# Layer 0's routing logits as eight extra columns of the value and output projections, without the transposes of the second norm

## The chip, the core and the metric

The kernel runs on one core of a Trainium2 chip. The metric is the device time of one execution in microseconds, the median over runs. TensorE is called PE here (its weight loads, which run beside matmuls, PEld), VectorE DVE, ScalarE ACT, GpSimd POOL and SyncE SP; SP issues the DMAs of this kernel. Everything is float32 unless noted. An fp32 matmul leaves two matmul records in the trace, a transpose one.

## What is computed

The reference is a network of two layers on x of shape (2, 256, 56, 56). Only layer 0 matters here:

```python
x = x + attention(_ln_c(x), wq, bq, wk, bk, wv, bv, wo, bo)   # 7x7 windows, 8 heads of 32, _ln_c: over channels, eps 1e-6
t = _to_tokens(x)                                             # 6272 tokens of 256
u = _ln_t(t)                                                  # over channels, eps 1e-5
logits = u @ router_w.T                                       # 8 experts
...
rw, re = jax.lax.top_k(softmax(logits), 2)                    # renormalised
t = t + u + sum_e combine[:, e] * (gelu(u @ w1[e] + b1[e]) @ w2[e] + b2[e])
```

Layer 1, two 3x3 convolutions with ternary weights and a second mixture of experts, has its own code after it.

## The kernel before

`metaformer` is the path that runs; `general` stands behind a flag for inputs that it doesn't cover. The picture is cut into 14 strips (`STRIPS`, 2 images of 7) of 8 rows, a strip has 448 tokens (`NT`), that is 4 tiles (`NTT`) of 112 tokens (`TT`, 8 rows by 14 columns). The 256 channels `C` are two halves (`KC`) of 128 partitions, `E` is 8.

**The attention stage** loops over strips g, over 4 column tiles and 2 channel halves. Each of the 8 steps of a strip does `scores` (`sc`, a matmul per head, L1435, and a mask, L1444; ACT turns them into `ex`, L1454), then `attend` for the step before (`av`, L1464; DVE adds it to `acc`, L1474). Beside them generators advance by one `yield` a step:

- `project(g + 2)`: `token_stats` (DVE L700 to L705, POOL L713 to L715 gives `rstd` and `nmr`), `scaled` on ACT (`xn`, L721), eight transposes `px` (L1375) copied by ACT to `xc`, then the keys and queries `pj` (L1387; ACT writes `keys`, DVE `q_im`, L1399), one yield each, and the values `pv` (L1409) in two steps of two token tiles: two outputs of 112x256 in one PSUM tile, two DVE adds into `vals` (L1417).
- `leave(g - 1)`: `again` loads the strip a second time as `xr` and adds the output bias on POOL (L1320); the softmax's sums go out and come back by DMA (`sums`, `den`, `shares`, `rec`); DVE builds `oc` (L1520); then the last projection `pw` (L1533), two token tiles to a PSUM tile, and DVE adds it to `xr` (L1541). Then `norm0`, the second normalisation: `token_stats` of `xr`, ACT makes `u` (L721), eight transposes `pu` (L763) are copied by ACT to `ut` (L768), POOL adds u to xr (L770) and SP stores it as `x_mid`, eight matmuls `pl` of N = 8 (L777, 16 records) give the logits, and DVE copies them to `lgs` (L788).
- `settle0`, once both strips of a pair are normalised: DVE picks the best two experts (`first_max`: `most`, `hot`, `at`, L804 to L808), PE ranks tokens (`rk`, L836), DVE places them (`place`, `pos`, L858), and POOL scatters the rows to the experts' lists (`xs`, L860, 16 indirect DMAs a pair).

PSUM: `px`, `pj`, `pv`, `pw`, `pu`, `pl`, `rk` share one tag, `aux`, of pool `att_ps` with two buffers of one bank; `sc` and `av` have six banks of their own. A tile is handed out again when its last reader is done.

The order of instructions on each engine in the attention stage comes from the framework's scheduler. The expert stages are in an order written out by hand for SP, DVE, PE and ACT (`experts_in_order`). Strips 12 and 13 are "late": the rest of their `leave` runs between the tiles of layer 0's experts (`beside(j)` moves each generator by a step for each expert tile, and `routed_all` plans the remaining tiles after the last), and they use DVE where the other strips use POOL.

Of the kernel before, what the change touches and what calls it, by code (L numbers as in the profile page):

```python
# [20 lines left out]
P = 128  # L21
# [55 lines left out]
def bcast(ap, axis, shape):  # L77
    return ap.unsqueeze(axis).to_broadcast(shape)
# [551 lines left out]
def metaformer(ctx: ExitStack, tc: tile.TileContext, a: dict, out: bass.AP, flag):  # L630
# [88 lines left out]
    def scaled(dest, src, rstd, nmr):  # L719
        for t in range(NTT):  # L720
            nc.scalar.activation(  # L721
                dest[:, t, :],
                src[:, t, :],
                AF.Identity,
                bias=nmr[:, t : t + 1],
                scale=rstd[:, t : t + 1],
            )

    def routing(layer, wp, tp, ps):

        pre = f"L{layer}_ffn_"
        gate = wp.tile([P, KC, E], F32, tag="gate", name="gate")
        nc.sync.dma_start(gate, a[pre + "gate"].rearrange("(k p) e -> p k e", p=P))
        if layer == 1:
            gate_b = wp.tile([TT, E], F32, tag="gate_b", name="gate_b")
            nc.sync.dma_start(gate_b, a[pre + "gate_b"].partition_broadcast(TT))
# [11 lines left out]
        def norm(i, src, late=False):  # L748


            eng = nc.vector if late else small_eng
# [5 lines left out]
            scaled(u, src, rstd, nmr)  # L757
            yield
# [10 lines left out]
            if layer == 0:  # L769
                eng.tensor_tensor(src, src, u, ALU.add)  # L770
                nc.sync.dma_start(x_mid[i], src)
                yield
            lg = lgs[:, i * NTT : (i + 1) * NTT, :]
            pl = ps.tile([TT, NTT, E], F32, tag="pl" if layer else "aux", name="pl")
# [9 lines left out]
            if layer == 1:  # L784
                yield
                nc.vector.tensor_tensor(lg, pl, bcast(gate_b, 1, [TT, NTT, E]), ALU.add)
            else:
                nc.vector.tensor_copy(lg, pl)  # L788
# [209 lines left out]
        return norm, settle, tiles, gates, wgt, counted, sent  # L998
# [294 lines left out]
    with ExitStack() as st:  # L1293
# [22 lines left out]
        def again(g, eng):  # L1316

            xr[g] = tp.tile([TT, NTT, C], F32, tag="xr", name="xr")
            nc.sync.dma_start(xr[g], a["x_tok"][g])
            eng.tensor_tensor(xr[g], xr[g], bcast(bias["o"], 1, [TT, NTT, C]), ALU.add)  # L1320

# [3 lines left out]
        for n in "kqvo":  # L1325
            wt[n] = (aw if n == "o" else sw).tile([P, KC, C], F32, tag=f"w{n}", name=f"w{n}")
            nc.sync.dma_start(wt[n], a[f"L0_conv_w{n}"].rearrange("(k p) o -> p k o", p=P))
# [15 lines left out]
        nc.vector.tensor_copy(far_w.rearrange("p h w -> p (h w)"), far_f)  # L1343
        fits = aw.tile([TT, DEN], F32, tag="fits", name="fits")
# [5 lines left out]
        def fresh(s):  # L1350


            rows = slice(s * SR, (s + 1) * SR)
            nc.sync.dma_start(acc[:, :, rows, :], bcast(a["fresh"][:, rows, :], 1, [P, PAIRS, SR, W]))
# [8 lines left out]
        norm0, settle0, tiles0, gates0, wgt0, counted0, _ = routing(0, aw, tp, ps)  # L1363

        def project(g):
# [39 lines left out]
            for t in range(0, NTT, 2):  # L1405
                pj = ps.tile([TT, 2, C], F32, tag="aux", name="pv")
                for i in range(2):
                    for k in range(KC):
                        nc.tensor.matmul(  # L1409
                            pj[:, i, :],  # L1410
                            xc[:, k, (t + i) * TT : (t + i + 1) * TT],
                            wt["v"][:, k, :],
                            start=k == 0,
                            stop=k == KC - 1,
                        )
                for i in range(2):
                    nc.vector.tensor_tensor(  # L1417
                        vals[g % 3][:, t + i, :, 0::3, :],
                        pj[:, i, :].rearrange("p (j i d) -> p j i d", i=2, d=HD),
                        bias["v"].rearrange("p (j i d) -> p j i d", i=2, d=HD),  # L1420
                        ALU.add,
                    )
                yield
# [54 lines left out]
        def leave(g):  # L1478
# [50 lines left out]
            for t in range(0, NTT, 2):  # L1529
                pw = ps.tile([TT, 2, C], F32, tag="aux", name="pw")  # L1530
                for i in range(2):
                    for k in range(KC):
                        nc.tensor.matmul(  # L1533
                            pw[:, i, :],
                            oc[:, k, (t + i) * TT : (t + i + 1) * TT],
                            wt["o"][:, k, :],
                            start=k == 0,
                            stop=k == KC - 1,
                        )
                x = xr[g][:, t : t + 2, :]  # L1540
                nc.vector.tensor_tensor(x, pw, x, ALU.add)  # L1541
# [28 lines left out]

        fresh(0)
# [3 lines left out]
        finish(project(1))  # L1575
        before = None
# [105 lines left out]
    with mid:  # L1682
# [133 lines left out]
        with ExitStack() as both:  # L1816
# [45 lines left out]
            norm, settle, tiles, gates, wgt1, _, sent = routing(1, wp, tp, ps)  # L1862
# [115 lines left out]
def _laid_out(inputs):  # L1978
# [16 lines left out]
    for n in "qkvo":  # L1995
        a[f"L0_conv_w{n}"] = i[f"L0_conv_w{n}"].T
        a[f"L0_conv_b{n}"] = per_channel(i[f"L0_conv_b{n}"])
    a["L0_ffn_gate"] = i["L0_ffn_router_w"].T
# [61 lines left out]
```

## Time and profile before

| | us |
|---|---|
| median of 3 runs | 1784.78 |
| all runs | 1784.78, 1773.98, 1792.38 |
| profiled execution | 1925.16 (span 1923.3, granted clock 0.866) |
| busy over the span | PE 1564.4, PEld 1224.5, DVE 927.7, ACT 711.4, POOL 668.5 |
| scatters `xs` on POOL, both layers | 224 of 0.954 mean, 213.7 in all |

The profiled execution took 140.38 us more than the median of the runs. The profile of the whole span in 40 slices of 48 us:

```profile
PE   6999787797868875995789899966447999999964
...
PEclk9999798897968987997899999955557999999975
DMA  7032233212136676786653000033363787878758
```

Each digit is the busy share of a slice in tenths; PEclk is the clock that PE was granted. The attention stage covers the first 11 or 12 slices, layer 0's experts follow to about slice 19, then come the convolutions and layer 1's experts. The rows of the page that belong to the work around the change are groups of instructions: line, engine, operation, output and inputs, shapes, count; then busy time and mean ns of one; then the idle time just before them and what ended it.

```profile
L1409 PE MATMUL pv<-wv,xc 128*112 128x256 f32 x224 | 54.7, 388 | 0.0
L763 PE MATMUL pu<-ident,u 112*128 112x112 f32 x112 | 14.4, 270 | 0.0
L1541 DVE TENSOR_TENSOR xr<-pw,xr 112x512 f32<-112x512 f32 x28 | 19.3, 688 | 20.7 <-PE pw L1533 20.6
L1417 DVE TENSOR_TENSOR vals<-pv,bv 112x256 f32<-112x256 f32 x56 | 21.1, 417 | 27.2 <-PE pv L1409 27.2
```

Matmuls are pipelined, so the mean of one in such a row overstates what it holds PE for; the busy sum is the one to use.

### The profile page before, as it was taken

How to read it: one execution, taken by the hardware profiler on the slowest of the kernel's cores; microseconds unless marked ns; L12 is line 12 of the kernel's file. 1: busy time of each engine (PE TensorE's matmuls, PEld its weight loads, DVE VectorE, ACT ScalarE, POOL GpSimd, SP SyncE). 2: the span in 40 equal slices, each digit the busy share in tenths (PEclk: the TensorE clock that was granted, in tenths of full speed). 3: DMA queues.
4: the chain of work that ended last, by engine and by line, in shares of the span. 5: the costliest groups of instructions: out<-in, count | busy, mean ns of one | idle time of the engine just before them, and what ended most of it. 6: DMA issues, size and time to landing. Idle time of an engine off the chain costs nothing.

```text
span 1923.3 us, 26006 instructions
## 1 busy us (share of the span) xinstructions
PE 1564.4 (81%) x8709; PEld 1224.5 (64%) x8709; DVE 927.7 (48%) x2621; ACT 711.4 (37%) x1388; POOL 668.5 (35%) x676
## 2 busy tenths in 40 slices
PE   6999787797868875995789899966447999999964
PEld 3555454454537764784678788855335888888852
DVE  4467355354644425884787555575533111111136
ACT  3454332342323423542655352244223333333312
POOL 3013433414133564443355234235554222222210
PEclk9999798897968987997899999955557999999975
DMA  7032233212136676786653000033363787878758
GB/s 235 21 90 77 89 101 96 73 44 69 31 109 217 214 245 231 262 291 196 170 153 101 0 1 1 1 103 105 92 200 111 250 278 264 270 271 275 273 170 289
DMA packets 91887, 291.79 MB, mean 152 GB/s; under 512 B 20487, under 2 KB 35803, under 8 KB 80416
## 3 DMA queue, kind: packets, MB, share of 16 engines
q1 hardware_dynamic: 66736, 231.79, 38.3%
q0 software_dynamic: 21200, 51.82, 7.7%
q10 hardware_dynamic: 3808, 6.42, 1.0%
q8 instruction: 71, 1.16, 0.2%
q14 instruction: 72, 0.59, 0.1%
HBM read 218.51 MB, written 74.20 MB: 152 GB/s over the span
## 4 chain that ended last, share of the span: by engine, by line
PE 60%; DVE 14%; DMA 8%; issue 7%; another core or an unknown queue 6%; ACT 3%; POOL 2%; SPq 1%; DVEq 0%; POOLq 0%; ACTq 0%
PE ph L1091 13%; PE py L1108 12%; PE pc L1753 10%; PE av L1464 5%; PE pj L1387 4%; PE sc L1435 3%; DMA got<-ys 3%; PE pw L1533 3%; PE pv L1409 2%; PE pt L1059 2%; PE pl L777 2%; DVE t_stats L700 1%; DMA x_on<-x_mid 1%; PE pu L763 1%
## 5 line engine op out<-in xcount | busy, mean ns | idle before, releaser
L1091 PE MATMUL ph<-ut,w 128*128 128x256 f32 (+1 forms) x1472 | 317.6, 367 | 12.5 <-issue 6.5
L1108 PE MATMUL py<-w,h 128*128 128x256 f32 x1288 | 299.9, 381 | 2.4 <-issue 2.4
L1116 DVE TENSOR_TENSOR y<-py,w 128x512 f32<-128x512 f32 (+1 forms) x120 | 76.8, 640 | 441.7 <-PE py L1108 388.2
L1091 PEld LDWEIGHTS ph<-ut,w 128*128 128x128 f32 x1472 | 255.7, 198 | 43.9 <-issue 8.7
L860 POOL DMA_INDIRECT xs<-u,pos x224 | 213.7, 954 | 162.6 <-issue 97.7
L1753 PE MATMUL pc<-hi,wq 128*128 128x448 f32 x672 | 255.4, 381 | 16.6 <-ACT hi L1724 16.6
L1108 PEld LDWEIGHTS py<-w,h 128*128 128x128 f32 x1288 | 245.3, 192 | 36.0 <-issue 2.8
L1753 PE MATMUL pc<-lo,wq 128*128 128x448 f32 x672 | 254.1, 379 | 0.0
L1118 POOL DMA_INDIRECT ys<-y,dest x136 | 136.2, 1002 | 272.1 <-DVE dest L1066 186.4
L1098 ACT ACTIVATE h<-ph,w 128x256 f32<-128x256 f32 (+1 forms) x368 | 162.2, 448 | 129.0 <-PE ph L1091 74.1
L1454 ACT ACTIVATE ex<-sc 112x476 f32<-112x476 f32 (+3 forms) x224 | 116.7, 570 | 245.7 <-PE sc L1444 166.2
L1063 ACT COPY ut<-pt 128x512 f32<-128x512 f32 (+1 forms) x120 | 65.2, 543 | 308.3 <-PE pt L1059 246.0
L1474 DVE TENSOR_TENSOR acc<-av,acc 128x238 f32<-128x238 f32 (+3 forms) x224 | 87.6, 407 | 154.1 <-PE av L1464 72.4
L1464 PE MATMUL av<-ex,vals 112*64 112x238 f32 (+3 forms) x896 | 130.7, 413 | 28.6 <-DVE acc L1474 21.8
L1723 POOL TENSOR_TENSOR v<-pad 128x928 f32<-128x928 f32 (+1 forms) x56 | 98.3, 1761 | 159.4 <-DVE lo L1725 146.7
L1753 PEld LDWEIGHTS pc<-hi,wq 128*128 128x128 f32 x672 | 128.5, 192 | 31.8 <-ACT hi L1724 17.9
L1753 PEld LDWEIGHTS pc<-lo,wq 128*128 128x128 f32 x672 | 128.7, 192 | 15.4 <-DVE lo L1725 1.0
L1118 POOL DMA_INDIRECT ys<-y,to x81 | 84.4, 1042 | 127.3 <-DVE dest L1066 65.8
L1435 PE MATMUL sc<-q_im,keys 32*112 32x238 f32 (+3 forms) x896 | 99.3, 439 | 32.5 <-ACT ex L1454 21.2
L1464 PEld LDWEIGHTS av<-ex,vals 112*64 112x64 f32 x896 | 57.4, 146 | 83.5 <-issue 37.9
L713 POOL TENSOR_TENSOR t_rstd<-t_mv,eps 112x4 f32<-112x4 f32 x26 | 5.3, 203 | 280.9 <-DVE t_mv L702 280.9
L1724 ACT CAST hi<-v 128x928 fp32r<-128x928 f32 x56 | 54.1, 966 | 109.7 <-PE pc L1753 103.9
(237 smaller groups left out, 2286.1 us busy)
## 6 DMA issues: line engine op xcount, KB each, us to landing
w<-in_L_experts SPq DMA_DIRECT2D x64, 1154.0 KB
w<-in_L_experts SPq DMA_DIRECT2D x56, 641.0 KB
xg<-xs SPq DMA_DIRECT2D x97, 260.0 KB
got<-ys SPq DMA_DIRECT2D x28, 896.0 KB
acc<-in_fresh SPq DMA_DIRECT2D x14, 896.0 KB
xt<-in_x_tok SPq DMA_DIRECT2D x14, 448.0 KB
xr<-in_x_tok SPq DMA_DIRECT2D x14, 448.0 KB
rec<-shares SPq DMA_DIRECT2D x28, 224.0 KB
```

The source lines that it names most:

```text
L860: w = nc.gpsimd.indirect_dma_start(xs[:, :], bass.IndirectOffsetOnAxis(ap=pos[:, j, t0 + t : t0 + t + 1], axis=0), us[t // NTT][:, t % NTT ...
L1091: nc.tensor.matmul(ph[:, :g], w1[:, k, f * P : (f + 1) * P], d["ut"][:, k, :g], start=k == 0, stop=k == KC - 1,)
L1098: nc.scalar.activation(d["h"][:, f, :g], ph[:, :g], AF.Gelu, bias=b1[:, f : f + 1])
L1108: nc.tensor.matmul(py[:, i, :], d["h"][:, f, i * P : (i + 1) * P], w2[:, f, :], start=f == 0, stop=f == NF - 1,)
L1118: o = nc.gpsimd.indirect_dma_start(ys[:, :], bass.IndirectOffsetOnAxis(ap=d["to"][:, i : i + 1], axis=0), y[:, i, :], None, bounds_check=T ...
L1387: nc.tensor.matmul(pj[:, :NT], wt[n][:, k, o * P : (o + 1) * P], xc[:, k, :], start=k == 0, stop=k == KC - 1,)
L1435: nc.tensor.matmul(sc[h // 2][:, h % 2, :nq], keys[g][p, c, tx * TT : (tx + 1) * TT], q_im[p, c, r0:r1, c0:c1], start=True, stop=False,)
L1454: nc.scalar.activation(e[:, :, :nq], sc[j][:, :, :nq], AF.Exp, scale=HD**-0.5)
L1464: nc.tensor.matmul(av[VW * i : VW * (i + 1), :nq], vals[g % 3][:, tx, 2 * c + j, 2 * i : 2 * i + 2, :].rearrange("p a d -> p (a d)"), ex[j ...
L1474: nc.vector.tensor_tensor(d, av[:, :nq].rearrange("p (h w) -> p h w", w=c1 - c0), d, ALU.add)
L1723: (nc.gpsimd if u else nc.vector).tensor_tensor(v[:, :, at : at + n, :], *r, op)
L1753: nc.tensor.matmul(pc[:, :NT], wq[:, k, c, dx * C + o * P : dx * C + (o + 1) * P], part[:, k, :, dx : dx + W], start=m == 0, stop=m == 2 * ...
```

## The change

Normalising u, projecting it and subtracting the mean can be exchanged: with g' the router's weights less their mean over channels, u . g' = rstd x (xr . g'), where xr = x + attention . wo + bo. The changed kernel adds up xr . g' from its three parts: x . g' comes as eight more columns of the value projection (`wv` becomes 264 columns wide; since that works on the first norm, the result is multiplied by the deviation `dev` = 1 / rstd), the attention's part as eight more columns of the output projection (`wo` wide likewise, its added columns are wo times g'), and bo . g' is a constant row `lg_b`. `gates_of_values` and `gates_of_output` compute the added columns at the start, from the gate, a second copy of wo in the other orientation and bo. In each strip `pv` and `pw` now take one token tile to a PSUM tile. ACT reads the eight columns of `pv`, DVE adds those of `pw`, POOL adds `lg_b` (DVE for the two late strips) and multiplies by `rstd`. For layer 0 the transposes `pu`, the copies `ut`, the matmuls `pl` and the copy to `lgs` are gone, and `norm` has one yield fewer; layer 1 keeps its own. Arrays on the host side only gain a view of wo as it comes.

```diff
@@ -729,9 +729,9 @@
     def routing(layer, wp, tp, ps):
 
         pre = f"L{layer}_ffn_"
-        gate = wp.tile([P, KC, E], F32, tag="gate", name="gate")
-        nc.sync.dma_start(gate, a[pre + "gate"].rearrange("(k p) e -> p k e", p=P))
         if layer == 1:
+            gate = wp.tile([P, KC, E], F32, tag="gate", name="gate")
+            nc.sync.dma_start(gate, a[pre + "gate"].rearrange("(k p) e -> p k e", p=P))
             gate_b = wp.tile([TT, E], F32, tag="gate_b", name="gate_b")
             nc.sync.dma_start(gate_b, a[pre + "gate_b"].partition_broadcast(TT))
         lgs = wp.tile([TT, NTOK, E], F32, tag="lgs", name="lgs")
@@ -748,6 +748,7 @@
         def norm(i, src, late=False):
 
 
+
             eng = nc.vector if late else small_eng
             rstd, nmr = yield from token_stats(tp, src, eps5, layer == 1 or late)
             row = rows[i] = tp.tile([TT, NTT, RW], F32, tag="u", name="u", bufs=U_BUFS[layer])
@@ -755,6 +756,14 @@
             eng.memset(row[:, :, R_EX + 1 :], 0.0)
             eng.tensor_copy(row[:, :, R_ID], ids[:, i * NTT : (i + 1) * NTT])
             scaled(u, src, rstd, nmr)
+            lg = lgs[:, i * NTT : (i + 1) * NTT, :]
+            if layer == 0:
+                eng.tensor_tensor(lg, lg, bcast(rstd, 2, [TT, NTT, E]), ALU.mult)
+                yield
+                eng.tensor_tensor(src, src, u, ALU.add)
+                nc.sync.dma_start(x_mid[i], src)
+                yield
+                return
             yield
             ut = tp.tile([P, KC, NT], F32, tag="ut", name="ut", bufs=1)
             for k in range(KC):
@@ -766,12 +775,7 @@
                         ident[:TT, :TT],
                     )
                 nc.scalar.copy(ut[:, k, :], pu[:, :NT])
-            if layer == 0:
-                eng.tensor_tensor(src, src, u, ALU.add)
-                nc.sync.dma_start(x_mid[i], src)
-                yield
-            lg = lgs[:, i * NTT : (i + 1) * NTT, :]
-            pl = ps.tile([TT, NTT, E], F32, tag="pl" if layer else "aux", name="pl")
+            pl = ps.tile([TT, NTT, E], F32, tag="pl", name="pl")
             for t in range(NTT):
                 for k in range(KC):
                     nc.tensor.matmul(
@@ -781,11 +785,8 @@
                         start=k == 0,
                         stop=k == KC - 1,
                     )
-            if layer == 1:
-                yield
-                nc.vector.tensor_tensor(lg, pl, bcast(gate_b, 1, [TT, NTT, E]), ALU.add)
-            else:
-                nc.vector.tensor_copy(lg, pl)
+            yield
+            nc.vector.tensor_tensor(lg, pl, bcast(gate_b, 1, [TT, NTT, E]), ALU.add)
             yield
 
         def settle(strips):
@@ -995,7 +996,7 @@
             nc.vector.tensor_tensor(held, below, since, ALU.mult)
             return where, held, name
 
-        return norm, settle, tiles, gates, wgt, counted, sent
+        return norm, settle, tiles, gates, wgt, counted, sent, lgs
 
     def experts(layer, FF, plans, ys, wp, tp, ps, at_tile=None):
 
@@ -1318,13 +1319,18 @@
             xr[g] = tp.tile([TT, NTT, C], F32, tag="xr", name="xr")
             nc.sync.dma_start(xr[g], a["x_tok"][g])
             eng.tensor_tensor(xr[g], xr[g], bcast(bias["o"], 1, [TT, NTT, C]), ALU.add)
+            lg = lgs0[:, g * NTT : (g + 1) * NTT, :]
+            eng.tensor_tensor(lg, lg, lg_b, ALU.add)
 
         load(0)
         load(1)
         wt = {}
         for n in "kqvo":
-            wt[n] = (aw if n == "o" else sw).tile([P, KC, C], F32, tag=f"w{n}", name=f"w{n}")
-            nc.sync.dma_start(wt[n], a[f"L0_conv_w{n}"].rearrange("(k p) o -> p k o", p=P))
+            wide = C + E if n in "vo" else C
+            wt[n] = (aw if n == "o" else sw).tile([P, KC, wide], F32, tag=f"w{n}", name=f"w{n}")
+            nc.sync.dma_start(
+                wt[n][:, :, :C], a[f"L0_conv_w{n}"].rearrange("(k p) o -> p k o", p=P)
+            )
         bias = {}
         for n in "kq":
             bias[n] = sw.tile([P, KC], F32, tag=f"b{n}", name=f"b{n}")
@@ -1341,6 +1347,47 @@
         nc.sync.dma_start(far_f, a["far"])
         nc.vector.tensor_copy(hot_w, hot_f)
         nc.vector.tensor_copy(far_w.rearrange("p h w -> p (h w)"), far_f)
+
+        wo_rows = parts[:, 2:].rearrange("p a j n -> p (a j n)")[:, : KC * C]
+        wo_rows = wo_rows.rearrange("p (k c) -> p k c", c=C)
+        bo = sw.tile([P, KC], F32, tag="bo_c", name="bo_c")
+        gate = sw.tile([P, KC, E], F32, tag="gate0", name="gate0")
+        nc.sync.dma_start(gate, a["L0_ffn_gate"].rearrange("(k p) e -> p k e", p=P))
+        lg_b = aw.tile([TT, NTT, E], F32, tag="lg_b", name="lg_b")
+
+        free = wt["v"][:, :, C:]
+
+        def gates_of_values():
+
+            pg = ps.tile([P, E], F32, tag="aux", name="pg")
+            for k in range(KC):
+                nc.tensor.matmul(pg, ones, gate[:, k, :], start=k == 0, stop=k == KC - 1)
+            mean = sw.tile([P, E], F32, tag="gate_mean", name="gate_mean")
+            nc.vector.tensor_scalar_mul(mean, pg, -1.0 / C)
+            nc.vector.tensor_tensor(free, gate, bcast(mean, 1, [P, KC, E]), ALU.add)
+
+        def gates_of_output():
+
+            nc.sync.dma_start(wo_rows, a["L0_conv_wo_rows"].rearrange("(k p) c -> p k c", p=P))
+            nc.sync.dma_start(bo, a["L0_conv_bo"])
+            po = ps.tile([P, KC, E], F32, tag="aux", name="po")
+            for k in range(KC):
+                for o in range(KC):
+                    nc.tensor.matmul(
+                        po[:, k, :],
+                        wo_rows[:, o, k * P : (k + 1) * P],
+                        free[:, o, :],
+                        start=o == 0,
+                        stop=o == KC - 1,
+                    )
+            nc.vector.tensor_copy(wt["o"][:, :, C:], po)
+            for k in range(KC):
+                nc.vector.tensor_scalar_mul(gate[:, k, :], free[:, k, :], bo[:, k : k + 1])
+            pb = ps.tile([TT, E], F32, tag="aux", name="pb")
+            for k in range(KC):
+                nc.tensor.matmul(pb, ones[:, :TT], gate[:, k, :], start=k == 0, stop=k == KC - 1)
+            nc.vector.tensor_copy(lg_b, bcast(pb, 1, [TT, NTT, E]))
+
         fits = aw.tile([TT, DEN], F32, tag="fits", name="fits")
         nc.vector.memset(fits, 0.0)
 
@@ -1360,7 +1407,7 @@
             nc.gpsimd.memset(t[:, :, :, 1:3, :], 1.0)
             vals.append(t)
         keys = {}
-        norm0, settle0, tiles0, gates0, wgt0, counted0, _ = routing(0, aw, tp, ps)
+        norm0, settle0, tiles0, gates0, wgt0, counted0, _, lgs0 = routing(0, aw, tp, ps)
 
         def project(g):
             s = g % NS
@@ -1402,25 +1449,29 @@
                             bias[n][:, o : o + 1],
                         )
                 yield
-            for t in range(0, NTT, 2):
-                pj = ps.tile([TT, 2, C], F32, tag="aux", name="pv")
-                for i in range(2):
-                    for k in range(KC):
-                        nc.tensor.matmul(
-                            pj[:, i, :],
-                            xc[:, k, (t + i) * TT : (t + i + 1) * TT],
-                            wt["v"][:, k, :],
-                            start=k == 0,
-                            stop=k == KC - 1,
-                        )
-                for i in range(2):
-                    nc.vector.tensor_tensor(
-                        vals[g % 3][:, t + i, :, 0::3, :],
-                        pj[:, i, :].rearrange("p (j i d) -> p j i d", i=2, d=HD),
-                        bias["v"].rearrange("p (j i d) -> p j i d", i=2, d=HD),
-                        ALU.add,
-                    )
-                yield
+            dev = sp.tile([TT, NTT], F32, tag="dev", name="dev")
+            nc.vector.reciprocal(dev, rstd)
+            for t in range(NTT):
+                pj = ps.tile([TT, C + E], F32, tag="aux", name="pv")
+                for k in range(KC):
+                    nc.tensor.matmul(
+                        pj,
+                        xc[:, k, t * TT : (t + 1) * TT],
+                        wt["v"][:, k, :],
+                        start=k == 0,
+                        stop=k == KC - 1,
+                    )
+                nc.vector.tensor_tensor(
+                    vals[g % 3][:, t, :, 0::3, :],
+                    pj[:, :C].rearrange("p (j i d) -> p j i d", i=2, d=HD),
+                    bias["v"].rearrange("p (j i d) -> p j i d", i=2, d=HD),
+                    ALU.add,
+                )
+                nc.scalar.activation(
+                    lgs0[:, g * NTT + t, :], pj[:, C:], AF.Copy, scale=dev[:, t : t + 1]
+                )
+                if t % 2:
+                    yield
 
         def scores(g, tx, c):
 
@@ -1526,19 +1577,20 @@
             if g < NS:
                 fresh(s)
             yield
-            for t in range(0, NTT, 2):
-                pw = ps.tile([TT, 2, C], F32, tag="aux", name="pw")
-                for i in range(2):
-                    for k in range(KC):
-                        nc.tensor.matmul(
-                            pw[:, i, :],
-                            oc[:, k, (t + i) * TT : (t + i + 1) * TT],
-                            wt["o"][:, k, :],
-                            start=k == 0,
-                            stop=k == KC - 1,
-                        )
-                x = xr[g][:, t : t + 2, :]
-                nc.vector.tensor_tensor(x, pw, x, ALU.add)
+            for t in range(NTT):
+                pw = ps.tile([TT, C + E], F32, tag="aux", name="pw")
+                for k in range(KC):
+                    nc.tensor.matmul(
+                        pw,
+                        oc[:, k, t * TT : (t + 1) * TT],
+                        wt["o"][:, k, :],
+                        start=k == 0,
+                        stop=k == KC - 1,
+                    )
+                x = xr[g][:, t, :]
+                nc.vector.tensor_tensor(x, pw[:, :C], x, ALU.add)
+                lg = lgs0[:, g * NTT + t, :]
+                nc.vector.tensor_tensor(lg, pw[:, C:], lg, ALU.add)
             yield
             yield from norm0(g, xr.pop(g), late)
             routed.append(g)
@@ -1568,11 +1620,13 @@
                 plans0.append(plan)
                 taken.append(n)
 
+        gates_of_values()
         fresh(0)
         finish(project(0))
         load(2)
         fresh(1)
         finish(project(1))
+        gates_of_output()
         before = None
         for g in range(len(STRIPS)):
             if g + 3 < len(STRIPS):
@@ -1859,7 +1913,7 @@
                 yield from residual(i)
                 yield from norm(i, XT[STRIPS[i]][:TT])
 
-            norm, settle, tiles, gates, wgt1, _, sent = routing(1, wp, tp, ps)
+            norm, settle, tiles, gates, wgt1, _, sent, _ = routing(1, wp, tp, ps)
 
             def fence():
 
@@ -1995,6 +2049,7 @@
     for n in "qkvo":
         a[f"L0_conv_w{n}"] = i[f"L0_conv_w{n}"].T
         a[f"L0_conv_b{n}"] = per_channel(i[f"L0_conv_b{n}"])
+    a["L0_conv_wo_rows"] = i["L0_conv_wo"]
     a["L0_ffn_gate"] = i["L0_ffn_router_w"].T
     a["L1_ffn_gate"] = i["L1_ffn_gate_w"]
     a["L1_ffn_gate_b"] = i["L1_ffn_gate_b"]
```

## The prediction

> **What bounds the kernel now.** I read the page's 40 slices first, then busy times by stretch, the chain of waits of the attention stage, and the timeline of one strip. The change touches the attention stage (about 20 to 570 us) and, for strips 12 and 13, the expert stage after it. Three strips and the start of a fourth, by stretch (us; then PE, PEld, DVE, ACT, POOL, granted clock, DMA share, GB/s):
>
> ```profile
> 76.60:102.80 26.20, 26.20 (x201) 14.31 (x201) 11.96 (x36) 12.84 (x25) 1.42 (x3) 1.00 0.07 20
> 102.80:135.34 32.54, 32.52 (x241) 19.28 (x241) 19.86 (x55) 15.73 (x31) 7.52 (x8) 1.00 0.32 95
> 135.34:169.46 34.12, 32.53 (x242) 19.27 (x241) 24.28 (x70) 17.49 (x34) 7.91 (x10) 0.98 0.26 76
> 169.46:219.83 50.37, 40.37 (x251) 23.71 (x250) 22.74 (x67) 15.35 (x29) 23.17 (x28) 0.78 0.35 102
> 50.00:560.00 510.00, 433.31 (x3072) 254.72 (x3066) 266.33 (x780) 189.70 (x368) 158.07 (x187) 0.88 0.24 71
> ```
>
> An ordinary strip is PE alone: 32.52 of 32.54 us busy at full clock. The last two rows show where PE isn't the bound: bursts of 16 POOL scatters after each pair of strips, named "another core or an unknown queue" in the chain (10.9% of 50 to 560). The change leaves them as they are. The chain holds the removed work itself:
>
> ```profile
> 143.65 3.45 PE pw L1533 x16
> ...
> 148.91 1.91 PE pv L1409 x8
> ...
> 152.48 1.91 PE pv L1409 x8
> ...
> 157.99 0.92 PE pu L763 x8
> ...
> 160.67 1.68 PE pl L777 x16
> 162.36 0.02 issue
> 162.38 0.20 DVE lgs L788
> ```
>
> The transposes pu and the logits pl cost PE 0.92 + 1.68 = 2.60 us a strip. In strips that settle a pair, the chain then goes over DVE to the routing, and this shows what a short stop costs (timeline; the bracket is the idle time ahead):
>
> ```profile
> 150.51 2.07 ACT L721 ACTIVATE u<-xr,t_nmr,t_rstd 112x256 f32<-112x256 f32 x4 [1.59 <-POOL t_nmr L715]
> 152.41 1.98 PE L1409 MATMUL pv<-wv,xc 128*112 128x256 f32 x8
> 162.86 1.95 DVE L805 TENSOR_TENSOR hot<-lgs,most 112x64 f32<-112x64 f32 x1
> 167.56 1.90 PE L1464 MATMUL av<-ex,vals 112*64 112x280 f32 x8 [1.59 <-DVE acc L1474]
> ```
>
> The routing block delays DVE's acc, PE stops 1.59 us, and its clock is 0.50 from 168 to 171: the eight av take 1.90 us instead of 1.09, the next eight pj 4.11 instead of 3.20.
>
> **What the skill says.** "TensorE: Matmul & The Clock Gate", What's actually happening, puts the half clock after an idle window of about 3.4 us. Here 1.59 us did it; the trace decides, so short stops are dear. "PSUM — Partial Sum Buffer", The four PSUM rules: a matmul's output stays within one bank of 512 fp32. Two tiles of 264 no longer share one, hence four PSUM tiles where there were two; the trace shows no more than the old 2 x 256. "VectorE: DVE Perf Modes", The TRN2 errata, charges a fixed cost per instruction; the trace agrees: 112x256 takes 0.417, 112x512 0.688, 112x32 0.188 us. "ScalarE: Activation LUTs", What ACT_TABLE_LOAD costs, gives an activation 186 ns + 0.833 ns a column + 93 ns a pointer operand: 585 ns for 256 columns and two pointers, against 590 in the trace; for the new 112x8 read with one pointer my estimate is 0.29 us.
>
> **Part by part, 14 strips.** *Removed:* per strip 2.60 us of PE, two ACT copies ut of 0.535, one DVE copy of 0.188.
>
> *Eight columns more.* pv and pw are 16 records each a strip. From pj (448 columns, 0.400 us) and pv (256, 0.239) a column costs 0.84 ns: 32 x 8 x 0.84 ns = 0.22 us. Net PE: 2.60 - 0.22 = 2.38 us.
>
> *DVE* changes four pw adds of 0.417 for two of 0.688, gains four 112x8 adds (about 0.19, by the 112x32 copy) and a reciprocal (0.2), loses the copy: +0.29 + 0.76 + 0.20 - 0.19 = +1.06 us. It is 60 to 70% busy, so the sum is hidden; the order is not. *POOL* gains two ops on 112x32 at 0.20 to 0.25 (t_rstd's row): 0.45, hidden outside the bursts, where it must be bounded at 0 to 0.45. On SP the order stays but for two loads after the second fresh. The step that adds u to xr and issues the x_mid DMA keeps its place; settling comes one step earlier (pl to u, about 2.7 us), and with it on POOL the pair's 16 scatters of 0.95 to 1.25, ahead of the same next-strip statistics as before; at nothing, or one step's 2.7 us a burst either way, which the reserve holds.
>
> *A wait in place of the removed one.* Each pv bank is now freed by a DVE add and an ACT read, and the pool has two banks for all of this. In the instruction order of the changed kernel, ACT's first two reads stand behind the four u activations, which wait for POOL's t_nmr, which waits for DVE's statistics of xr. Queued behind: those reads, then the next exponentials; waiting for them: PE's second pv pair, with sc and av behind it. In DVE's order, in the first image, statistics of xt also come after pw's adds. Worked on the strip above: DVE's last t_mv moves from 148.87 to about 150.7; POOL's chain is 1.5 (148.91 to 150.48), so u starts at 152.4, ends 154.5, two reads end at 154.9. PE wants the bank at 152.41 + 0.35 for a wait on pw's fourth bank + 0.2 for columns + 0.5 for late values = about 153.4: a stop of 1.4 to 1.5. Gain 2.38 - 1.45 - 0.35 - 0.3 = about 0.3 us. In the second image no xt statistics intervene, the stop is some 0.4, the gain 2.
>
> *The routing block moves.* It came after pl, ahead of acc. Now it comes right after t_nmr, and its first operation waits for POOL's lg x rstd, about 1.8 us, with DVE's acc and vals queued behind. That lies inside the stop just counted. In exchange the old stop goes: 1.59 plus 0.81 + 0.91 of slow clock, of which I count 2.5 to 3.
>
> *Sum of the loop:* six settled strips, three in each image: 3 x -2.8 and 3 x -4 = -20; other strips, three at -0.3 and three at about -2, minus the first strip of each image, which finds no statistics in its way, -1 = -8. Where a burst follows, PE waits for the scatters and a gain ahead of it is hidden; I take a quarter of these 28 for that, +7. Together -21.
>
> *Start:* gate sums, wo times gate and bo times gate add 16 small PE records of 0.1 to 0.25, some 2.5 us, and 257 KB by DMA. The gate's DMA is issued ahead of PE's first work but behind the masks; at worst PE waits for two landings (near 2 us each). wo_rows lies in the buffer that rec takes a strip later, free by then. Bounds 0 to +6, taken +3.
>
> *Expert stage:* strips 12 and 13 (and the tail of 11) lose 2.60 of PE each, 7 in all, and their routing comes a tile earlier (4 to 5 us). But 720 to 768 is bound by scatters and the fetch behind them, PE being busy for 25.86 of 48. Bounds 0 to -12, taken -5.
>
> *Reserve* for POOL's two ops, DVE's later backlog and the moved scatters: 0 to +10, taken +5. **Total: -21 + 3 - 5 + 5 = -18 us.** The profiled execution took 1925.16 us (span 1923.3), 140 over the median, most of it where clock and scatters are slow; my terms lie in stretches at full clock, so I carry the difference, not a ratio: 1784.78 - 18 = **1766**.
>
> **Rivals.** *A, above* (42%): 1752 to 1778. *B, PE's saving comes through whole* (20%): u's reads come in time, since ACT is busy for only 17.49 of 34.12 us. 14 x 2.38 = 33, + 9 for the old stops, - 3 for the start: -39, or 1746. For it: strips at 32.52 of 32.54. Against it: ACT's order. *C, a swap* (12%): stop and column cost take the whole 2.38, routing gains only what the start costs: about 1784. *D, slower* (26%): the same bank wait on pv reaches 2.4 us and lets the clock fall to 0.5, as 1.59 us did at 165.97, for another 1.6 us. Then a strip costs 2.4 + 1.6 - 2.38 = +1.6 us, and with POOL's t_nmr behind a scatter (0.95 to 1.25 us) +2. In 10 strips +16 to +20, start +3: 1805 (1790 to 1820). It decides where stop plus slow clock exceed 2.38 us; my 1.45 is 0.15 short of the stop that did it. That the change doesn't do what it says I exclude: pu and pl are gone for layer 0 from PE's order.
>
> **Numbers.** 1% of 1784.78 is 17.8 us, about what a measurement tells from no change: faster is below 1767, slower above 1802.6. A lies 60% under 1767, B wholly, C between, D 65% above 1802.6. Faster 0.45, same 0.37, slower 0.18. The range 1740 to 1803 leaves out a quarter of B and half or more of D.
>
> **What will show it.** PE per ordinary strip: 30.1 busy, in a span between 30.2 (B) and 32.3 (A). The second pv with idle ahead "<-ACT lgs" of 1 to 2 us in first-image strips, less in the second; over 2, with clock 0.5 after it, is D. The acc stop of 1.59 gone in settled strips. Scatter bursts as long as before. I'm wrong if pv finds its bank free, if DVE's routing makes a stop larger than the old, or if the bursts move and lengthen.

## The result and the profile after

The changed kernel takes 1796.01 us (median of 20 runs, 1786.82 to 1803.32), the kernel before 1777.55 (20 runs, 1765.93 to 1792.38): a ratio of 1.0094, 95% interval 1.0074 to 1.0114, so some 17 us slower where 18 faster were forecast.

The first profile of the kernel before took 140 us more than that median, and so did its runs in one later series (1923.9 us), so every ratio here is to the kernel before in the same series. Its second profile (1770.96 us, span 1769.1) stands here beside the changed kernel's. The stops that no semaphore ended, 28 us in the bursts of the first profile, are not in the second. Part 1 of the page of the changed kernel:

```profile
span 1796.5 us, 25530 instructions
## 1 busy us (share of the span) xinstructions
PE 1530.1 (85%) x8389; PEld 1191.2 (66%) x8389; DVE 937.5 (52%) x2715; ACT 711.2 (40%) x1416; POOL 679.4 (38%) x700
```

Stretches from one pw to the next; first before, second profile (columns as in the prediction):

```profile
112.00:143.80 31.80, 31.80 (x240) 19.21 (x240) 20.44 (x58) 15.77 (x30) 7.53 (x8) 1.00 0.32 97
178.20:211.60 33.40, 32.33 (x250) 19.57 (x250) 22.78 (x68) 15.77 (x30) 22.16 (x24) 1.00 0.46 135
```

then after:

```profile
116.05:149.59 33.54, 31.57 (x218) 17.40 (x217) 20.47 (x63) 15.65 (x32) 7.95 (x10) 1.00 0.28 84
186.05:224.40 38.35, 31.90 (x226) 18.03 (x226) 23.27 (x74) 15.64 (x32) 24.87 (x30) 0.95 0.42 122
```

PE is busy for about as long as before though 2.60 us of its work are gone, and the strips are longer. The waits of PE from 50 to 497 us, in all, times, longest; before (second profile), then after:

```profile
PE av L1464 <- DVE acc L1474: 10.6, 9, 2.0
PE pw L1533 <- DVE q_im L1399: 10.4, 6, 4.5
PE pw L1533 <- DVE oc L1520: 7.7, 2, 7.3
```

```profile
PE pw L1583 <- DVE q_im L1446: 15.8, 4, 6.5
PE pw L1583 <- DVE oc L1571: 14.3, 4, 7.7
PE av L1515 <- DVE acc L1525: 8.6, 6, 2.3
PE pv L1457 <- ACT lgs L1470: 4.3, 6, 1.4
```

The stops are at pw, which waits for oc and q_im, not at the second pv, where the prediction put them (4.3 us in all). An account of PE from the start to the last av, from the records and the granted clock (work: busy time less half of what was busy at half clock, so at full clock):

| us | before, second | after | difference |
|---|---|---|---|
| last av ends | 497.7 | 518.2 | +20.5 |
| work | 431.6 | 419.7 | -11.9 |
| idle | 49.2 | 67.9 | +18.7 |
| lost to half clock | 16.9 | 30.6 | +13.7 |

pu and pl were 30.2 us of the work before; some 18 came back as other work. The records show the start (2.5 us for the new weights) and the wider pv and pw in it; short waits between records that count as busy may be the rest, which isn't shown. From the last av to layer 0's last expert tile both take 299, so nothing was gained there.

### The profile page after: what moved, and what is told of

It reads as the page before. It is cut to its first block, busy times and chain, and to the rows that moved or that the text cites. A ratio compares the mean times of both kernels' runs of the same rounds, so it can differ in the third digit from the quotient of the medians.

```text
span 1796.5 us, 25530 instructions
## 1 busy us (share of the span) xinstructions
PE 1530.1 (85%) x8389; PEld 1191.2 (66%) x8389; DVE 937.5 (52%) x2715; ACT 711.2 (40%) x1416; POOL 679.4 (38%) x700
## 4 chain that ended last, share of the span: by engine, by line
PE 36%; DVE 7%; DMA 6%; issue 2%; ACT 2%; POOL 1%; SPq 0%; POOLq 0%; DVEq 0%; ACTq 0%
PE pc L1807 12%; PE ph L1092 10%; PE py L1109 10%; DMA got<-ys 3%; PE pt L1060 1%; DMA out<-o_out 1%; DVE x_on L1173 1%; PE pl L781 1%; PE pu L772 1%; DVE t_stats L700 1%; POOL x_on L1177 1%; PE pu L1184 1%; DMA xs<-u,pos 1%; DMA x_on<-x_mid 1%; ACT ut L777 0%
## 5 line engine op out<-in xcount | busy, mean ns | idle before, releaser
L1092 PE MATMUL ph<-ut,w 128*128 128x256 f32 (+1 forms) x1472 | 309.5, 361 | 11.1 <-DMA w<-in_L_experts 11.1
L1092 PEld LDWEIGHTS ph<-ut,w 128*128 128x128 f32 x1472 | 251.3, 195 | 39.5 <-DMA w<-in_L_experts 13.2
L861 POOL DMA_INDIRECT xs<-u,pos x224 | 217.7, 972 | 119.7 <-issue 56.0
L1515 PE MATMUL av<-ex,vals 112*64 112x238 f32 (+3 forms) x896 | 126.3, 402 | 10.5 <-DVE acc L1525 9.2
L1486 PE MATMUL sc<-q_im,keys 32*112 32x238 f32 (+3 forms) x896 | 103.1, 433 | 5.8 <-ACT ex L1505 5.6
L1583 PE MATMUL pw<-wo,oc 128*112 128x264 f32 x224 | 70.3, 474 | 36.0 <-DVE oc L1571 19.6
```

The lines of the kernel that those rows point to most:

```text
L861: w = nc.gpsimd.indirect_dma_start(xs[:, :], bass.IndirectOffsetOnAxis(ap=pos[:, j, t0 + t : t0 + t + 1], axis=0), us[t // NTT][:, t % NTT ...
L1092: nc.tensor.matmul(ph[:, :g], w1[:, k, f * P : (f + 1) * P], d["ut"][:, k, :g], start=k == 0, stop=k == KC - 1,)
L1486: nc.tensor.matmul(sc[h // 2][:, h % 2, :nq], keys[g][p, c, tx * TT : (tx + 1) * TT], q_im[p, c, r0:r1, c0:c1], start=True, stop=False,)
L1515: nc.tensor.matmul(av[VW * i : VW * (i + 1), :nq], vals[g % 3][:, tx, 2 * c + j, 2 * i : 2 * i + 2, :].rearrange("p a d -> p (a d)"), ex[j ...
```

## The experiments

Ratios are to the kernel before in the same series, with 95% intervals. State of the theories at the outset: D, the bank of pv held by ACT (the prediction's); S, the smaller PSUM tiles; R, the removed work had covered a latency. P came later: the place of the routing.

**Another profile of before.** 

> The kernel before, unchanged, for a second profile, since the first one took 140 us more than the median. All theories expect about 1778 us; if the first profile's 14 idle stretches of PE in the attention stage that no semaphore of the trace ends (about 28 us) were an accident of that execution, they are gone here and the attention stage ends near 520 us instead of 569.

It took 1770.96 us and ended the attention stage at 497.7.

**The smaller tiles.** One token tile to a PSUM tile in the kernel before, for pw and pv:

```diff
-            for t in range(0, NTT, 2):
-                pw = ps.tile([TT, 2, C], F32, tag="aux", name="pw")
+            for t in range(NTT):
+                pw = ps.tile([TT, C], F32, tag="aux", name="pw")
...
-                x = xr[g][:, t : t + 2, :]
+                x = xr[g][:, t, :]
                 nc.vector.tensor_tensor(x, pw, x, ALU.add)
```

> The kernel before with one token tile to a PSUM tile for pv and pw, as in the change, and four DVE adds of 112x256 in place of two of 112x512 for pw; logits as before (pu, ut, pl kept). Theory S (the smaller PSUM tiles and the extra DVE instructions are what costs): 10 to 20 us slower than before. Theory R (the removed PE work had covered the DMA round trip of the softmax's sums and the products oc behind it, so its removal gains nothing, and the start and later order cost): within 5 us of before. Theory D of the prediction (bank of pv held by ACT): within 3 us of before, since ACT reads none of it.

1.0115 (1.0079 to 1.0151): as much as the whole change. Then each half alone, and the DVE adds alone (two of 112x256 for each PSUM tile of two):

> The kernel before with one token tile to a PSUM tile for pw alone (four DVE adds in place of two); pv as before. Split of both cost 1.0115. Theory S-pw (pw's four tiles turn over two banks that DVE has to empty between its other work, and PE stops in the middle of the group, since oc has just kept DVE busy): 12 to 20 us slower than before, 1.007 to 1.012. Theory S-pv (the pv tiles are it): within 5 us of before.

> The kernel before with one token tile to a PSUM tile for pv alone; pw as before, and as many DVE instructions as before. Theory S-pw: within 5 us of before (0.997 to 1.003). Theory S-pv: 10 to 20 us slower.

> The kernel before with pw in two PSUM tiles of two as it was, but each emptied by two DVE adds of 112x256 in place of one of 112x512: 0.29 us more of DVE a strip, 4 us in all, no other change. If the fixed cost of more DVE instructions is what the split costs: 8 to 20 us slower, about as the split of pw. If it is the banks' turnover: within 5 us of before.

pw alone 1.0070 (1.0048 to 1.0091), pv alone 1.0009 (0.9989 to 1.0029), the adds 1.0032 (1.0011 to 1.0054). So it is pw, and by the middle values a little under half of it comes with the two more adds on DVE. One pw in the kernel before (second profile), then in the run with pw split:

```profile
143.76 3.62 PE L1533 MATMUL pw<-wo,oc 128*112 128x256 f32 x16
```

```profile
142.33 1.03 PE L1532 MATMUL pw<-wo,oc 128*112 128x256 f32 x4
143.28 0.66 PE L1435 MATMUL sc<-q_im,keys 32*112 32x238 f32 x2
143.87 2.43 PEld L1532 LDWEIGHTS pw<-wo,oc 128*112 128x112 f32 x12 [0.32 <-DVE xr L1540]
```

The bracket names DVE's add, but PE does not stand still here: between the first PSUM tile of pw and the other three, its order now has two sc, which in the kernel before came after pw. From first to last record such a group takes 4.4 to 4.5 us instead of 3.6, with the change 4.6, and no gap within it is over 0.02 us. That the smaller tiles make the scheduler place sc there is what the two orders suggest; no run tests it. In strips without sc inside, the group takes 3.7 to 4.0 us at full clock. The cost shows behind the group: what waits for pw comes later, as the table of the ring below shows.

**ACT or DVE for pv's columns**, in the changed kernel:

```diff
-                nc.scalar.activation(
-                    lgs0[:, g * NTT + t, :], pj[:, C:], AF.Copy, scale=dev[:, t : t + 1]
-                )
+                nc.vector.tensor_scalar_mul(lgs0[:, g * NTT + t, :], pj[:, C:], dev[:, t : t + 1])
```

> The changed kernel with the eight columns of pv read by DVE (times dev) instead of ACT, so that no bank of pv waits behind the normalised rows on ACT. Theory D: the gain of the change appears, 15 to 30 us faster than the changed kernel (about 0.985 of before or less). Theory R: about as the changed kernel, within 5 us (1.006 to 1.012 of before), since pw then waits for oc all the same. Theory S: slower than the changed kernel by a few us, four more DVE instructions a strip.

1.0056 (1.0027 to 1.0086): some 7 us better than the change, two fifths of the loss, though the two intervals overlap. The same edit beside the queries on ACT (below) gives 0.47% within one series, clear of noise. But it isn't D as predicted. The stops at pv are 4.3 us with ACT's read and 3.0 with DVE's. The two long ones, 1.41 us each and then 1.19, stay at the same work, and the trace of the changed kernel shows why:

```profile
394.20 2.35 POOL L763 TENSOR_TENSOR xr<-xr,u 112x1024 f32<-112x1024 f32 x1 [0.59 <-ACT u L721]
394.83 1.80 DVE L806 TENSOR_TENSOR hot<-rest,most 112x64 f32<-112x64 f32 x1
396.81 0.42 DVE L1464 TENSOR_TENSOR vals<-pv,bv 112x256 f32<-112x256 f32 x1
397.26 0.27 ACT L1470 ACTIVATE lgs<-pv,dev 112x8 f32<-112x8 f32 x1 [2.29 <-DVE vals L1464]
397.58 1.90 PE L1457 MATMUL pv<-wv,xc 128*112 128x264 f32 x4 [1.41 <-ACT lgs L1470]
```

ACT's read is short and waits 2.29 us itself, for DVE's vals, which stands behind a routing operation under POOL's add. What is shorter in the profile is the way to pw: strip 0 to 1 takes 32.0 us instead of 33.5, and PE's stop ahead of pw is 0.5 instead of 2.0.

**The removed work put back** beside the change (pu, ut, pl in norm, results unused):

> The changed kernel with the removed work put back beside it: the eight transposes pu, the two ACT copies ut, the eight matmuls pl (with eight columns of the identity in place of the gate) and a DVE copy of their result, which nothing reads; one more step as before. It adds 2.60 us of PE a strip, 36 us in all. If the change's saving is real and something else costs more (S, D): 20 to 36 us slower than the changed kernel (1.021 to 1.03 of before). Theory R: the work fits into the waits of pw for oc and q_im, so 0 to 8 us slower than the changed kernel (1.009 to 1.014 of before).

1.0149 (1.0118 to 1.0181). The edit brings back the step of norm as well, so the run to set beside it is the changed kernel with that step alone, 1.0058 below: 36 us of PE work then cost 0.9%, about 16 us. In the two profiles strip 0 to 1 takes 33.1 us with the work and 33.0 without; what it costs lies in later strips. And the opposite, the removal alone in the kernel before:

```diff
+            if layer == 0:
+                nc.vector.tensor_copy(lgs[:, i * NTT : (i + 1) * NTT, :], u[:, :, :E])
+                yield
+                eng.tensor_tensor(src, src, u, ALU.add)
+                nc.sync.dma_start(x_mid[i], src)
+                yield
+                return
```

> The kernel before with pu, ut and pl taken out and nothing put in: the logits are the first eight channels of the normalised row, copied by DVE, so the tokens go to other experts and the output is not the reference's; PSUM tiles, wv, wo and the start are as before. It leaves out 2.60 us of PE a strip, 36 us in all. Theory R (pu and pl filled the time of the sums' round trip and of oc): 5 to 14 us faster, 0.992 to 0.997 of before, with pw waiting longer for oc and q_im than the 18.5 us of before. If PE bounds the strips: 25 to 36 us faster, 0.980 to 0.986.

Its logits are no logits: they are the first eight channels of u, so tokens go to other experts. 1.0053 (1.0028 to 1.0078), slower: R had expected 5 to 14 us of gain, so R alone isn't it. What else the edit does is take a yield out of norm, as the change does. Two runs separate them: the removal with an empty yield in its place, and the kernel before with pl in pu's step, all its work kept.

> The removal alone (pu, ut and pl out of the kernel before, logits from the first eight channels of the normalised row, so the output is not the reference's), with one empty step more, so that routing begins as many steps after the norm as before. The removal with the step gone too was 1.0053 of before. Theory P (the routing's new place, on POOL's add and ahead of acc and vals, is what costs): 10 to 30 us faster than that run, 0.985 to 0.998 of before. Theory R (pu and pl had covered the sums' round trip): within 5 us of that run, 1.003 to 1.008.

> The kernel before with pl in the same step as pu, so that norm has one yield fewer and routing starts a step earlier, with all of its work kept. Theory P: 5 to 20 us slower than before, 1.003 to 1.011. Theory R: within 4 us of before.

The removal with its step kept: 0.9990 (0.9976 to 1.0004). The step gone with the work kept: 1.0046 (1.0024 to 1.0068). These two stand beside a kernel before of 1923.9 us. There the profile of the removal takes 27.0 us from sums to oc in strip 2 to 3, against 11.7 in the second profile of before, so a gain of PE in such strips can't show, and 0.9990 alone doesn't settle what the removal is worth. The ordinary strips do: strip 0 to 1 takes 31.2 us in both profiles of the removal, against 31.8 with the work, and PE stops there ahead of pw (table below). So in the kernel before 2.60 us less of PE shorten a strip by 0.6, and the step costs. In the changed kernel:

```diff
                 nc.sync.dma_start(x_mid[i], src)
                 yield
+                yield
                 return
```

> The changed kernel with one empty step more in layer 0's norm, so that routing begins as many steps after the norm as in the kernel before; nothing else. Theory P (the routing's new place costs): 4 to 12 us faster than the changed kernel in the same call. Theory R (only the removed work as cover, and the bank turnover): within 3 us of it.

> The changed kernel itself, for the comparison in one call. 1.0094 of before again if the call runs on a chip like the first one; if on one where the kernel before takes 1924 us, anything from 1.000 to 1.012, since there PE stops longer in the bursts of scatters and small losses ahead of a burst are hidden.

1.0058 (1.0037 to 1.0079) against 1.0101 (1.0073 to 1.0130) beside it: 8.5 us between the medians, in P's range. The attention stage ends at 502.7 us, 15.5 earlier; the rest is lost again in the expert stage, which takes 309 instead of 299 in that profile, and why isn't shown. The timeline shows the path. Changed kernel (POOL, then SP's issues):

```profile
193.89 1.21 POOL L861 DMA_INDIRECT xs<-u,pos  x1 [0.19 <-DVE pos L859]
...
198.85 2.39 POOL L763 TENSOR_TENSOR xr<-xr,u 112x1024 f32<-112x1024 f32 x1
...
201.26 0.31 SPq L764 DMA_DIRECT2D x_mid<-xr  x1
...
204.39 0.31 SPq L1320 DMA_DIRECT2D xr<-in_x_tok  x1
204.79 1.20 SPq L1543 DMA_DIRECT2D sums<-acc  x2
```

With the step back:

```profile
197.16 2.36 POOL L763 TENSOR_TENSOR xr<-xr,u 112x1024 f32<-112x1024 f32 x1 [0.47 <-ACT u L721]
199.54 0.31 SPq L764 DMA_DIRECT2D x_mid<-xr  x1
200.83 1.21 POOL L862 DMA_INDIRECT xs<-u,pos  x1 [1.31 <-DVE pos L860]
```

Without the step, ranking is done sooner and the first four scatters slip in ahead of POOL's add of u to xr. That add releases x_mid; the next load of xr waits for x_mid (3.13 us here and in before), and the sums stand behind that load in SP's queue. From there it is a ring that closes at pw: the next strip's oc needs the sums' round trip. The ring, measured from one pw to the next:

| us | pw to x_mid | to sums | to oc | oc | to pw | whole | PE's stop |
|---|---|---|---|---|---|---|---|
| before (second), strip 0 to 1 | 11.7 | 3.7 | 9.6 | 4.7 | 2.2 | 31.8 | 0 |
| after, 0 to 1 | 12.2 | 4.8 | 10.2 | 5.1 | 1.1 | 33.5 | 2.0 |
| before (second), 2 to 3 (scatters) | 11.6 | 3.5 | 11.7 | 4.7 | 1.8 | 33.4 | 1.0 |
| after, 2 to 3 | 15.2 | 3.5 | 11.5 | 6.9 | 1.1 | 38.3 | 6.5 |
| removal alone, 0 to 1 | 11.6 | 3.5 | 9.7 | 5.1 | 1.1 | 31.2 | 0.7 |
| before (second), 1 to 2 | 11.6 | 4.0 | 12.5 | 4.7 | 1.8 | 34.4 | 1.1 |
| pw split alone, 1 to 2 | 12.6 | 4.0 | 12.5 | 4.7 | 1.8 | 35.5 | 0.9 |
| after with the step, 2 to 3 | 12.2 | 4.1 | 11.6 | 5.1 | 1.1 | 34.1 | 0.3 |

Even before, the ring was 2.2 us short of PE's work at best: oc ended 2.2 us ahead of pw, part of which q_im takes, and in the other two stretches of before PE already stops. Hence 2.60 us less of PE buy 0.6 in the row of the removal, and the split of pw, which lengthens the first part of the ring by 1.0 us, lengthens the strip by 1.1.

**Moving pw** one step later, alone and with DVE for pv's columns:

```diff
             if g < NS:
                 fresh(s)
             yield
+            yield
             for t in range(NTT):
```

> The changed kernel with one more yield between the products oc and the projection pw in leave, so that pw comes one step later in PE's order, behind one more sc, av and the first pv pair, and its place after the end of the strip is again that of before. Theory R (with pu and pl gone PE reaches pw before the sums' round trip, oc and q_im are done, stops there for about 30 us in all and runs at half clock after it): the stops at pw fall under 12 us, and it is 10 to 25 us faster than the changed kernel (0.995 to 1.004 of before). If the stops only move to pv or sc: within 5 us of the changed kernel (1.007 to 1.012). Theory D: within 5 us of the changed kernel, the bank of pv being held as before.

> The changed kernel with both earlier edits: pw one step later and the eight columns of pv read by DVE. In the run with pw later alone pw's groups took 3.8 us again, but PE stopped 21 us for exponentials, which stood on ACT behind a read of pv's columns that waited for DVE's adds behind the routing block. Theory M (several short covers are used up, each removal uncovers the next): the stops for exponentials fall under 8 us, and it is 10 to 25 us faster than the run with pw later alone, 1.000 to 1.008 of before. Theory D alone (ACT's read is the whole loss): 0.98 to 0.995 of before.

1.0166 (1.0121 to 1.0211) and 1.0105 (1.0072 to 1.0138). The group is short again (3.8 us), but the stops move, as here in the run with pw later alone:

```profile
160.69 2.34 POOL L763 TENSOR_TENSOR xr<-xr,u 112x1024 f32<-112x1024 f32 x1 [1.44 <-ACT u L721]
160.98 2.13 DVE L809 TENSOR_TENSOR hot<-order,at 112x64 f32<-112x64 f32 x1
163.48 0.27 ACT L1470 ACTIVATE lgs<-pv,dev 112x8 f32<-112x8 f32 x1 [2.62 <-DVE vals L1464]
164.26 1.20 PE L1486 MATMUL sc<-q_im,keys 32*112 32x238 f32 x6 [3.34 <-ACT ex L1505]
```

A routing operation that takes 0.22 us elsewhere takes 2.13 while POOL adds; DVE's vals follow it, ACT's read follows those, the exponentials follow the read, and PE stops 3.34 us. The theories that these edits were for had expected a gain of both. In the profile of the first, oc ends 4.9 us ahead of pw in strip 0 to 1 instead of 1.1: a later pw is a longer ring.

**Queries on ACT** instead of DVE (`nc.scalar.activation(..., AF.Identity, bias=...)` in place of `tensor_scalar_add`, in project): in the changed kernel, with DVE for pv's columns too, with the step back as well, and in the kernel before.

> The changed kernel with the queries written out of PSUM by ACT instead of DVE (ACT does the keys so already), 1.34 us less of DVE a strip and 1.26 more of ACT. If pw's group is long because its second PSUM tile waits for the bank that q_im, behind oc on DVE, has to free: pw's groups fall from 4.6 to about 3.9 us in ordinary strips, the 15.8 us of pw's stops at q_im go, and it is 10 to 25 us faster than the changed kernel, 0.995 to 1.004 of before. If oc itself, after the round trip, is what pw waits for: the stops carry oc's name, and it is within 5 us of the changed kernel. ACT's exponentials may come later by up to 0.63 us a step, which would take back a few us.

> The changed kernel with the queries on ACT and the eight columns of pv on DVE: both engines get what the other had. If bank turnover on DVE and ACT is the whole loss, 15 to 30 us faster than the changed kernel, 0.990 to 1.000 of before; if the sums' round trip remains as the next wall, no better than the run with the queries on ACT by more than 7 us (the gain that reading by DVE had alone).

> The changed kernel with the queries on ACT, pv's columns on DVE and one empty step more ahead of the routing. Theory P: another 5 to 15 us faster than without that step (0.998 of before), so 0.989 to 0.996. Theory R: within 4 us of it.

> The kernel before with the queries on ACT and nothing else. pw has two tiles to a PSUM tile here, its groups take 3.7 us in ordinary strips and its stops at q_im are 10.4 us in the attention stage. If that edit helps by itself, about those stops: 4 to 12 us faster, 0.993 to 0.998. If it only mends what the smaller PSUM tiles broke: within 3 us of before, and then the changed kernel with the same relief (1.0027) is no faster than the kernel before with it.

1.0027 (1.0011 to 1.0043), 0.9980 (0.9965 to 0.9995), 0.9924 (0.9904 to 0.9943) and 0.9977 (0.9962 to 0.9992). q_im sat between oc and pw on DVE, in the ring; after the edit pw's stops at q_im are 0.7 us, those at oc 13.0. The third beats the kernel before by 0.76%; against the kernel before with the same queries on ACT, in the same series, it is 1911.63 to 1920.15 us. These two stand beside a before of 1923.9, the first two beside 1776.49.

## Why the prediction was wrong, step by step

- *"An ordinary strip is PE alone"*, and with it "Net PE: 2.38 us" a strip as what the waits are taken from. This failed. PE was busy throughout and yet not the only bound: the ring above took as long as PE to within 2.2 us. The view for it was there, in how shortly before pw oc ended (2.2 us in strip 0 to 1 of the first profile too), but it was read for busy shares only. Measured: 0.6 us from strip 0 to 1, and 0.9990 for the removal with its step kept, about 2 us where 14 x 2.38 = 33 were counted, though beside the longer before. In the changed kernel the same work costs about 16 us of its 36; why it is worth more there is open.
- *The moved step*, "at nothing, or one step's 2.7 us a burst either way", ahead of "the same next-strip statistics as before", while the add of u to xr "keeps its place". Failed: the scatters passed not those statistics but POOL's add of u, with x_mid, SP's queue and the sums behind it. 8.5 us in the changed kernel, 0.46% alone.
- *"The sum is hidden; the order is not"* on DVE. Half right: the cost was booked as 0.35 us for pw's fourth bank; the group grew by about 0.9, through two sc inside it and the columns, not through a wait, and splitting pw alone cost 0.70%, 12 us. The count of 1.06 us of DVE left out that a later end of pw makes the ring longer.
- *The wait of pv for ACT*: there, but neither in the place nor for the reason given. It was put at 1.4 to 1.5 us in first-image strips and 0.4 in the second image. In the trace six stops add up to 4.3 us: four of 0.36 to 0.45 and two of 1.41, both in the second image, where DVE's routing operation under POOL's add holds everything behind it. That the long ones have the size forecast is luck. Reading on DVE gave back 0.4%, most of it not at pv.
- *Settled strips*: the stop at acc did not go. Where 2.5 to 3 us were counted as won, a settled strip of the changed kernel shows this:

```profile
160.20 1.82 DVE L806 TENSOR_TENSOR hot<-rest,most 112x64 f32<-112x64 f32 x1
163.93 1.02 PE L1515 MATMUL av<-ex,vals 112*64 112x238 f32 x8 [1.64 <-DVE acc L1525]
```

The clock was 0.50 from 165.7 to 172.5 after it.
- *Start*, +3: pw of strip 0 comes 4.2 us later. *Expert stage*, -5: 0.
- *That a stop of 1.59 us brings the clock down*: half right. The time lost to half clock grew by 13.7 us. But the length of a stop doesn't decide it: a stop of 1.24 us up to 318.2 in the second profile of before was followed by 0.50 within 0.3 us, one of 1.97 up to 149.6 in the changed kernel by 16 us more at full clock. So nothing follows from 1.45 being "0.15 short of the stop that did it". Rival D had the sign right and the place (pv) wrong.

One by one, pw's split costs 0.70%, the step 0.43 to 0.46% and ACT's read 0.4%, some 1.5% together against 0.94% measured; the removal gives something back, and how much of the rest is overlap isn't shown. Not tried: issuing the sums ahead of xr's load on SP. From x_mid to sums the table has 3.5 to 4.8 us, so my estimate is up to 3 us out of the ring.

## What to carry to other kernels

A strip in which an engine is 100% busy can at the same time be held by a ring of DMAs and small operations of the same length, as strip 0 to 1 was here; before counting removed work as gain, measure that ring from one strip to the next and its slack where it closes. When a step moves, list what now stands ahead of whom on every in-order queue, DMA issue included, and follow each until it returns to the bounding engine. A smaller PSUM tile can also change the order in which a scheduler interleaves matmuls; look at where the group ends, not only at its own work.

## What the runs showed of the hardware

Under POOL's add of 112x1024 (2.34 to 2.36 us), DVE operations with two inputs in SBUF took longer: a routing operation 2.13 us in the run with pw later and 1.80 in the changed kernel instead of 0.22, ending 0.08 us after the add in both; in strip 2 to 3 of the changed kernel one of the eight oc 2.35 instead of 0.62, and the eight 6.4 instead of 4.6.

The clock record has 1.00 and 0.50 alone in the attention stage, and stretches at 0.50 last 3.41 us or multiples of it. Stops of PE of 1.24 and 1.79 us (up to 318.2 in the second profile of before, up to 383.7 in the changed kernel) were followed by such a stretch within 0.5 us, stops of 2.02 and 1.97 (up to 303.0 and up to 149.6) were not, for 15 us and more. What decides between them isn't shown.
